# Joined sums of the block products written to PSUM; inverse sums, scaling and norm placed in an element's first step

## The chip, the cores and the metric

The kernel runs on one core of a Trainium2 chip. The metric is the device time of one execution in microseconds (us), the median of several runs; lower is better.

The names of the engines in the profile: PE is TensorE (matrix products; PEld its weight loads), DVE is VectorE, ACT is ScalarE, POOL is GpSimd, and SP is the engine that issues nearly all DMAs. Each takes its instructions in the order in which the program lists them, so an instruction that waits holds up all those behind it on its engine.

## The reference

Two transformer blocks, one after the other, on x of 16 batch elements × 256 tokens × 256 channels, with a context of 256 × 192 for each element and a conditioning vector of 256. Both have a self-attention, a cross-attention to the context and a feed-forward network, each behind a modulated layer norm. The change lies in the first block's self-attention:

```python
def _attn(xq, ctx, wq, wkv, wo, bo):          # layer 0: 16 heads of 64
    q = _heads(xq @ wq)
    k, v = jnp.split(ctx @ wkv, 2, axis=-1)
    k, v = _heads(k), _heads(v)
    q, k = _rope(q, sq, cq), _rope(k, sk, ck)
    sim = jnp.einsum('bhnd,bhmd->bhnm', q, k) * DH ** (-0.5)
    a = jax.nn.softmax(sim, axis=-1)
    o = jnp.einsum('bhnm,bhmd->bhnd', a, v)
    return o.transpose(0, 2, 1, 3).reshape(...) @ wo + bo
attn_in = _adaln(x, cond, ...)                 # layer norm, then scale and shift from cond
x = _attn(attn_in, attn_in, sa_wq, sa_wkv, sa_wo, sa_bo) + x
```

## The kernel before

All of x stays in SBUF. The program runs phase by phase (self-attention, cross-attention and feed-forward of layer 0, then of layer 1), in each phase element by element, and an attention element in two steps, `s = 0` and `s = 1` (here: the first and the second step). One step handles half of the heads: two groups of four heads, `u = 2s` and `2s + 1`. The order of the instructions on every engine is written out by hand in the main loop; a small framework adds the waits that the data and the reuse of buffers need. PSUM is one tile `banks` of eight banks of 128 × 512 floats, addressed by number.

At the end of each step `scores` (line 679 for the products, 694 for the exponentials on ACT) computes the transposed scores of the next step: group 0 in banks 0 to 3, group 1 in banks 4 to 7, and exponentials of two banks at a time. The sums of the softmax are not taken on PE: DVE adds the two key tiles (`stage_t`, `both`, line 703), transposes in blocks of 32 (`stage_turn`, `squares`, line 709) and reduces (`stage_reduce`, `rows`, line 716). The division comes one element later: `late` is the element before. `sum_up` (line 720 on) finishes its sums on PE with the matrix `fold`, inverts them on DVE (line 725), writes them to DRAM (`sums_seen`, line 728) and reads them back by four DMAs spread over 32 partitions each (`spread`, line 731); `scale` (line 740) multiplies the unscaled outputs by them on POOL, four instructions of 128 × 512. Then `fold_inner` (line 1031) prepares sums of blocks for the output projection, seven block products in place of eight, which `finish_folded` runs in the second step in banks 4 and 5, adding to x on DVE (lines 1045 to 1054).

The projections of queries and keys for the next step are also made as seven block products in place of eight (`seven`, from `by_seven` on: all elements but the first), over combinations of weights (`fold_projections`) and of token halves (`fold_tokens`, four POOL instructions, lines 593 to 596). Products 1 and 5 are started in banks 0 and 1 right behind the scores (`begin_seven`), ACT copies bank 0 into bank 2 (line 616), and further products are accumulated: banks 0, 1 and 2 are `first`, `fifth` and `chain`. Two states of `chain` are kept by ACT in SBUF (`keep_sum`, line 624, tile `kept`), and DVE later adds `fifth` to each (`add_fifth`, line 628). `rotate` applies the rotary embedding to one block (head half, token half): two DVE products with the cosines and sines (line 637, tiles `m0` and `m1`, two buffers each) and two POOL instructions that combine them into `qk` (line 643). A step has four rotations.

The layer norm of an element is split in time over three elements: `prepare_moments` (statistics on DVE; POOL's power, line 356), `prepare_norm` (two DVE scalings, line 364, two block transposes, line 374, four DMAs to DRAM, line 379, and two POOL additions of the bias to x, line 452) for the element `third`, `prepare_fetch` (four DMAs back, line 389) for `after`, and `prepare_input` (modulation by ACT, line 422, and POOL, line 426). `layer0_values` computes the values of the next element (`nxt`) in four banks, copied out by ACT (line 508).

Of the kernel before, what the change touches and what calls it, by code (L numbers as in the profile page):

```python
# [10 lines left out]
F32 = mybir.dt.float32  # L11
I32 = mybir.dt.int32
AF = mybir.ActivationFunctionType
ALU = mybir.AluOpType
AX = mybir.AxisListType

P = 128
N = 256
D = 256
# [4 lines left out]
NT = N // P  # L24
# [19 lines left out]
def fast(ctx: ExitStack, tc: tile.TileContext, a: dict, out: bass.AP, flag):  # L44
# [215 lines left out]
        return src.rearrange("(c p) m -> p c m", p=p)  # L260

    def broadcast_row(src, tag, name):
        t = wpool.tile([P, D], F32, tag=tag, name=name)
        nc.sync.dma_start(out=t, in_=src.partition_broadcast(P))
        return t

    def wtile(shape, tag, name, bufs=1):
        return wpool.tile(shape, F32, tag=tag, name=name, bufs=bufs)
# [219 lines left out]
    def layer0_values(job):  # L488

        w, key, kT = job["phase"]["w"], job["key"], job["kT"]  # L490
        job["v"] = work.tile([P, NT, H * 64], F32, tag="v", name=f"v_{key}")
        halves = [slice(half * 512, (half + 1) * 512) for half in range(2)]
        places = [[bank(6 - 2 * t + half, 512) for half in range(2)] for t in range(NT)]
        for t in range(NT):
            for pv, cut in zip(places[t], halves):
                for k in range(1 if job["cross"] else 2):
                    product(pv, kT[:, k, t * P : (t + 1) * P], w["wv"][:, k, cut], k == 0, k == 1)
        for t in range(NT if job["cross"] else 0):
            for g in range(2):
                for half, (pv, cut) in enumerate(zip(places[t], halves)):  # L500
                    r, m = slice(64 * half, 64 * half + 64), slice(64 * g, 64 * g + 64)
                    nc.tensor.matmul(  # L502
                        pv[m], kT[r, 1, t * P + 64 * g : t * P + 64 * g + 64], w["wv"][r, 1, cut],
                        start=False, stop=True,
                    )
        for t in range(NT):
            for pv, cut in zip(places[t], halves):
                nc.scalar.copy(job["v"][:, t, cut], pv)  # L508
# [78 lines left out]
    def fold_tokens(job, eng):  # L587

        b = [[job["hT"][:, k, t * P : (t + 1) * P] for t in range(NT)] for k in range(KC)]
        t1, t2, t3, t4 = (  # L590
            t for i in range(2) for t in wtile([P, 2, P], "bv", f"tokens{i}_{job['key']}", 2).rearrange("p i n -> i p n")
        )
        eng.tensor_tensor(t1, b[0][1], b[0][0], ALU.subtract)
        eng.tensor_tensor(t2, b[1][1], t1, ALU.subtract)
        eng.tensor_tensor(t3, b[1][1], b[0][1], ALU.subtract)
        eng.tensor_tensor(t4, b[1][0], t2, ALU.subtract)
        job["tokens"] = {1: b[0][0], 2: b[1][0], 3: b[1][1], 4: t4, 5: t1, 6: t2, 7: t3}
# [26 lines left out]
        nc.scalar.copy(kept, bank(2, 4, P))  # L624
        return kept

    def add_fifth(kept):
        nc.vector.tensor_tensor(kept, bank(1, 4, P), kept, ALU.add)  # L628

    def rotate(job, s, e, t, src):  # L630

# [572 lines left out]
    for i, (j, s) in enumerate(steps):  # L1204
# [123 lines left out]
        elif layer0:  # L1328
            then = attention(i + 1, 0)
            if leaving and s == 1 and nxt["kind"] == "ffn":  # L1330
                fold_input_weights(nxt["phase"], nc.gpsimd)
            if by_seven(then):
                ahead = then
                first, fifth, chain = (bank(n, 4, P) for n in range(3))
                for p in range(2):
                    stage_t(job, 2 * s, p)
                stage_turn(job, 2 * s)
                if late is not None and s == 1:
                    fold_inner(late, nc.gpsimd, 7, 6)
                if make_mod:  # L1340
                    make_mod["mod"] = make_mod["make_mod"](6)
                stage_t(job, 2 * s + 1, 0)
                layer0_sums(job, 2 * s, 4, (0,))
                seven(*ahead, 2, first)
                rotate(*ahead, 0, 0, first)
                seven(*ahead, 6, chain)
                two = keep_sum(*ahead, 0)
                if late is not None and s == 0:
                    sum_up(late, 6)
                stage_reduce(job, 2 * s)  # L1350
                layer0_sums(job, 2 * s, 4, (1,))
                stage_t(job, 2 * s + 1, 1)
                layer0_sums(job, 2 * s + 1, 5, (0,))
                seven(*ahead, 7, chain)
                three = keep_sum(*ahead, 1)
                layer0_sums(job, 2 * s + 1, 5, (1,))
                seven(*ahead, 4, chain)
                add_fifth(three)
                rotate(*ahead, 1, 1, three)
                seven(*ahead, 3, fifth)  # L1360
                add_fifth(two)
                rotate(*ahead, 0, 1, two)
                rotate(*ahead, 1, 0, chain)
                if leaving and s == 0:
                    load_phase(job["p"] + 1, "last")
                stage_turn(job, 2 * s + 1)
                if late is None or s == 0:
                    stage_reduce(job, 2 * s + 1)
            else:
                stage_t(job, 2 * s, 0)  # L1370
                stage_t(job, 2 * s, 1)
                stage_turn(job, 2 * s)
                rotary(then, 0, 0)
                stage_t(job, 2 * s + 1, 0)
                rotary(then, 0, 1)
                if late is not None and s == 1 and then:
                    fold_inner(late, nc.gpsimd, 7, 6)
                if late is not None and s == 0:
                    sum_up(late, 6)
                if make_mod:  # L1380
                    make_mod["mod"] = make_mod["make_mod"](6)
                stage_t(job, 2 * s + 1, 1)
                rotary(then, 1, 0)
                rotary(then, 1, 1)
                if leaving and s == 0:
                    load_phase(job["p"] + 1, "last")
                for e in range(2):
                    layer0_sums(job, 2 * s + e, 4 + e if then else e)
                stage_reduce(job, 2 * s)
                stage_turn(job, 2 * s + 1)  # L1390
                stage_reduce(job, 2 * s + 1)
            if late is not None and s == 1:
                if then:
                    finish_folded(late, (4, 5), (lambda: stage_reduce(job, 3)) if by_seven(then) else None)
                else:
                    finish(late, 7)
            if late is not None and s == 0:
                if job["p"] == 0 and not nxt["cross"]:
                    fold_tokens(nxt, nc.gpsimd)
                scale(late)  # L1400
                if nxt["kind"] == "attn":
                    fold_inner(late, nc.gpsimd, 5, 2, 1)
            if nxt["kind"] == "attn" and s == 0:
                layer0_values(nxt)
            if s == 0:
                prepare_moments(third)
                context_moments(third)
                prepare_fetch(after)
            else:
                if job["p"] == 0 and job["b"] == 0:  # L1410
                    fold_projections(job["phase"], 1, nc.vector)
                prepare_norm(third)
                prepare_context(third)
                prepare_input(after)
                if job["b"] == 0:
                    fold_weights(job["phase"])
        else:
            then = attention(i + 1, 1)
            at = 4 * s
            if s == 0:  # L1420
                prepare_fetch(after)
            if then:
                stage_a(then[0], then[1], at)
            if nxt["kind"] == "ffn" and s == 1:
                ffn_products(nxt, 0, at)
            for e in range(2):
                layer1_sums(job, s, e, at + 2 + e)
                if s == 1:
                    finish(prev, at + 1, (e,))
                elif nxt["kind"] == "attn":  # L1430
                    layer1_values(nxt, at + 1, e)
            if s == 0 and prev["kind"] == "attn":
                invert(prev)
                show_sums(prev)
                normalize(prev)
            if s == 0:
                prepare_moments(third)
            else:
                prepare_norm(third)
                prepare_input(after)  # L1440
                if job["cross"] and job["b"] == 5:
                    fold_input_weights(phases[job["p"] + 1], nc.gpsimd)
# [624 lines left out]
```

## Time and profile before

| | |
|---|---|
| median of 3 runs | 2209.86 us (2208.7 to 2212.47) |
| the profiled execution | 2207.08 us, span 2205.3 us |
| busy share of the span | PE 98%, PEld 67%, DVE 82%, POOL 60%, ACT 42% |
| granted TensorE clock | 0.999 |
| chain that ended last | PE 74%, DVE 15%, POOL 5%, issue 3% |
| self-attention of layer 0, elements 1 to 12 | second step 22.8 us, first step 20.3 us, from the starts of `begin_seven` |

Busy shares are means over the whole span. A group line names line, engine, operation, output and inputs, shape, count, then durations. A line of the timeline has start, length, engine, line, operation and count; the bracket gives the idle time of the engine just before and what ended it. A line of the chain of waits has start, length and the work that the end waited for at that time. The difference between the time of an execution and its span (1.8 us here) lies around the profiled instructions.

### The profile page before, as it was taken

What the parts mean: (1) busy time and instruction counts of PE and PEld (TensorE: products, weight loads), DVE (VectorE), ACT (ScalarE), POOL (GpSimd) and SP (SyncE); (2) the same over time, 40 slices, a digit from 0 to 9 for tenths busy, and PEclk for the clock granted to TensorE, in tenths of its full rate; (3) what the DMA queues carried; (4) which work ended last, traced back from release to release, by engine and by line L of the source; (5) the groups of instructions that cost most, each with busy time, mean ns of one, the idle gap of its engine ahead of it and who ended that gap; (6) DMA issues with size and microseconds to landing.
All of it is one profiled execution on the core that took longest, in us unless ns stands there. A gap on an engine that the chain in (4) does not pass through costs nothing.

```text
span 2205.3 us, 116296 instructions
## 1 busy us (share of the span) xinstructions
PE 2152.0 (98%) x52992; PEld 1471.8 (67%) x52992; DVE 1805.7 (82%) x3176; ACT 923.7 (42%) x1452; POOL 1332.6 (60%) x1362
## 2 busy tenths in 40 slices
PE   9899999999999999999999999999999999999999
PEld 5666677677676666665666666877665656666888
DVE  6998898898998999888888887775677777777875
ACT  3333433433343333323333333443566666665342
POOL 5867776776677776776767676673223223225763
PEclk9999999999999999999999999999999999999999
DMA  5111001101123221212121123221211232223221
GB/s 191 25 28 37 23 23 38 27 23 28 41 54 92 58 73 41 59 35 65 34 54 46 36 56 94 68 45 32 57 41 42 51 96 56 59 57 80 69 67 38
DMA packets 307054, 118.06 MB, mean 54 GB/s; under 512 B 243364, under 2 KB 289784, under 8 KB 306424
## 3 DMA queue, kind: packets, MB, share of 16 engines
q1 hardware_dynamic: 306008, 110.02, 20.2%
q8 instruction: 416, 6.82, 1.3%
q14 instruction: 86, 0.70, 0.1%
q10 hardware_dynamic: 544, 0.52, 0.1%
HBM read 77.14 MB, written 33.29 MB: 50 GB/s over the span
## 4 chain that ended last, share of the span: by engine, by line
PE 74%; DVE 15%; POOL 5%; issue 3%; DMA 1%; ACT 1%; SPq 0%; DVEq 0%; POOLq 0%; ACTq 0%
PE banks L82 47%; PE banks L679 13%; PE banks L751 7%; PE banks L770 5%; DVE m L637 5%; DVE both L703 3%; DVE squares L709 2%; PE banks L535 1%; PE banks L502 1%; POOL folded L956 1%; POOL folded L1031 1%; POOL raw L740 1%; DVE rows L716 1%; DVE kept L628 1%; ACT pr L694 1%
## 5 line engine op out<-in xcount | busy, mean ns | idle before, releaser
L694 ACT ACTIVATE pr<-banks 128x1024 f32<-128x1024 f32 x576 | 492.5, 936 | 487.7 <-PE banks L679 380.0
L703 DVE TENSOR_TENSOR both<-pr 128x512 f32<-128x512 f32 x256 | 267.2, 1061 | 55.8 <-ACT pr L694 52.4
L679 PE MATMUL banks<-qk 32*64 32x256 f32 x8192 | 255.1, 380 | 26.6 <-DVE x L1054 17.9
L643 POOL TENSOR_TENSOR qk<-m,m 128x256 f32<-128x256 f32 x240 | 194.7, 840 | 131.3 <-DVE m L637 126.4
L564 POOL TENSOR_TENSOR qk<-m,m 128x512 f32<-128x512 f32 x136 | 184.8, 1380 | 134.5 <-DVE m L556 115.4
L679 PEld LDWEIGHTS banks<-qk 32*64 32x64 f32 x8192 | 187.3, 132 | 98.5 <-DVE x L1054 25.6
L751 PE MATMUL banks<-pr,v 128*32 128x256 f32 x4096 | 244.6, 379 | 0.0
L556 DVE TENSOR_TENSOR m<-banks,rope 128x512 f32<-128x512 f32 x272 | 172.3, 679 | 48.8 <-POOL qk L564 45.8
L751 PEld LDWEIGHTS banks<-pr,v 128*32 128x32 f32 x4096 | 131.1, 110 | 72.4 <-ACT pr L694 0.7
L761 ACT COPY raw<-banks 128x512 f32<-128x512 f32 x128 | 75.1, 587 | 247.5 <-PE banks L751 241.4
L740 POOL TENSOR_TENSOR raw<-raw,spread 128x512 f32<-128x512 f32 x128 | 169.2, 1355 | 13.9 <-DMA spread<-sums_seen 12.4
L812 POOL TENSOR_TENSOR oT<-oT,spread 128x256 f32<-128x256 f32 x64 | 45.7, 736 | 206.1 <-DVE spread L811 206.1
L709 DVE STREAM_TRANSPOSE squares<-both 128x1024 f32<-128x1024 f32 x128 | 158.9, 1241 | 3.4
L716 DVE TENSOR_REDUCE rows<-squares 128x32 f32<-128x1024 f32 x128 | 154.5, 1207 | 1.7
L452 POOL TENSOR_TENSOR x<-x,bo_b 128x256 f32<-128x256 f32 x96 | 72.7, 778 | 120.2 <-DVE xh L364 120.2
L508 ACT COPY v<-banks 128x512 f32<-128x512 f32 x128 | 70.4, 593 | 170.4 <-PE banks L82 107.0
L1031 POOL TENSOR_TENSOR folded<-raw,raw 128x512 f32<-128x512 f32 x90 | 135.7, 1535 | 2.4
L770 PE MATMUL banks<-pr,wide_v 128*32 128x256 f32 x2048 | 134.3, 379 | 0.0
L82 PE MATMUL banks<-hT,wq_ca 128*32 128x256 f32 x2048 | 133.9, 379 | 0.0
L987 DVE TENSOR_TENSOR x<-banks,x 128x256 f32<-128x256 f32 (+2 forms) x150 | 79.7, 531 | 63.8 <-PE banks L82 57.7
L356 POOL TENSOR_TENSOR rstd<-ve,neg_half 128x2 f32<-128x2 f32 x95 | 68.6, 722 | 99.3 <-DVE ve L354 95.8
L679 PE MATMUL banks<-q,k 32*64 32x256 f32 x4096 | 127.7, 381 | 0.0
(266 smaller groups left out, 4569.6 us busy)
## 6 DMA issues: line engine op xcount, KB each, us to landing
turned<-blocks SPq DMA_DIRECT2D x380, 64.0 KB
fetched<-turned SPq DMA_DIRECT2D x380, 64.0 KB
spread<-sums_seen SPq DMA_DIRECT2D x128, 128.0 KB
x<-in_x SPq DMA_DIRECT2D x16, 256.0 KB
fetched_c<-turned_c SPq DMA_DIRECT2D x64, 64.0 KB
cT<-in_ctx_turned SPq DMA_DIRECT2D x16, 256.0 KB
out<-x SPq DMA_DIRECT2D x15, 256.0 KB
ctx<-in_ctx SPq DMA_DIRECT2D x16, 192.0 KB
```

The costliest lines, as they stand in the source:

```text
L82: nc.tensor.matmul(out[cut], lhsT[:, cut], rhs, start=start, stop=stop, **more)
L556: nc.vector.tensor_tensor(m, pq, rope[:, s : s + 1, :].to_broadcast([P, 2, N]), ALU.mult)
L564: nc.gpsimd.tensor_tensor(r, x, y, (ALU.subtract, ALU.add)[out])
L643: nc.gpsimd.tensor_tensor(r[:, :, t * P : (t + 1) * P], cos[:, i], sin[:, 1 - i], (ALU.subtract, ALU.add)[i])
L679: nc.tensor.matmul(banks[64 * g : 64 * g + 64, at + h, t * N : (t + 1) * N], lhs, rhs, start=(half == 0 and (t == 0 or job["layer"] == 1)) ...
L694: nc.scalar.activation(pr[:, one], sc[:, one], AF.Exp, scale=0.125 if job["layer"] == 0 else 0.25)
L703: nc.vector.tensor_tensor(job["both"][:, 2 * p : 2 * p + 2, :], pr[:, :, 0, :], pr[:, :, 1, :], ALU.add)
L709: nc.vector.transpose(job["squares"].rearrange("p b k -> p (b k)"), job.pop("both").rearrange("p h n -> p (h n)"))
L716: nc.vector.tensor_reduce(job["rows"][:, u, :], job.pop("squares"), AX.X, ALU.add)
L740: nc.gpsimd.tensor_tensor(part, part, spread[:, u : u + 1, :].to_broadcast([P, 2, N]), ALU.mult)
L751: nc.tensor.matmul(o[32 * h : 32 * h + 32, half, :], v[:, t, col : col + 32], prs[h // 2][:, h % 2, t, :], start=(t == 0), stop=(t == NT - 1),
L770: nc.tensor.matmul(o[32 * h : 32 * h + 32], v[:, t, 4 * c + h, 32 * e : 32 * e + 32], prs[h // 2][:, h % 2, t, :], start=(t == 0), stop=(t ...
```

## The change

- `add_fifth` writes its result to a PSUM bank (7 or 3) and `rotate` reads it there, no longer from `kept` in SBUF.
- In the steps with seven products, `sum_up` of the element before, `fold_tokens` of the next one and `scale` go from the end of the first step to its beginning: `sum_up` and `fold_tokens` ahead of `stage_turn`, `scale` behind the first rotation. `prepare_moments` goes to the same place, and `prepare_norm` from the second step to the end of the first.
- The reduction of the first group goes behind the rotations.
- `layer0_values` uses banks 4, 5, 6, 7 in this order, before 6, 7, 4, 5. The token sums have four buffers, before two.

```diff
 def broadcast_row(src, tag, name):
-        t = wpool.tile([P, D], F32, tag=tag, name=name)
+        t = wpool.tile([P, D], F32, tag=tag, name=name, bufs=4 if tag == "bv" else 2)
...
 def layer0_values(job):
-        places = [[bank(6 - 2 * t + half, 512) for half in range(2)] for t in range(NT)]
+        places = [[bank(4 + 2 * t + half, 512) for half in range(2)] for t in range(NT)]
...
 def fold_tokens(job, eng):
-            t for i in range(2) for t in wtile([P, 2, P], "bv", f"tokens{i}_{job['key']}", 2).rearrange("p i n -> i p n")
+            t for i in range(2) for t in wtile([P, 2, P], "bv", f"tokens{i}_{job['key']}", 4).rearrange("p i n -> i p n")
...
-    def add_fifth(kept):
-        nc.vector.tensor_tensor(kept, bank(1, 4, P), kept, ALU.add)
+    def add_fifth(kept, at):
+        out = bank(at, 4, P)
+        nc.vector.tensor_tensor(out, bank(1, 4, P), kept, ALU.add)
+        return out
...
             if by_seven(then):
                 for p in range(2):
                     stage_t(job, 2 * s, p)
+                if s == 0:
+                    if late is not None:
+                        sum_up(late, 6)
+                    if not nxt["cross"]:
+                        fold_tokens(nxt, nc.gpsimd)
                 stage_turn(job, 2 * s)
...
                 rotate(*ahead, 0, 0, first)
+                if s == 0:
+                    prepare_moments(third)
+                    if late is not None:
+                        scale(late)
                 seven(*ahead, 6, chain)
                 two = keep_sum(*ahead, 0)
-                if late is not None and s == 0:
-                    sum_up(late, 6)
-                stage_reduce(job, 2 * s)
                 layer0_sums(job, 2 * s, 4, (1,))
...
                 seven(*ahead, 4, chain)
-                add_fifth(three)
-                rotate(*ahead, 1, 1, three)
+                rotate(*ahead, 1, 1, add_fifth(three, 7))
                 seven(*ahead, 3, fifth)
-                add_fifth(two)
-                rotate(*ahead, 0, 1, two)
+                rotate(*ahead, 0, 1, add_fifth(two, 3))
                 rotate(*ahead, 1, 0, chain)
                 if leaving and s == 0:
                     load_phase(job["p"] + 1, "last")
+                stage_reduce(job, 2 * s)
                 stage_turn(job, 2 * s + 1)
...
             if late is not None and s == 0:
-                if job["p"] == 0 and not nxt["cross"]:
-                    fold_tokens(nxt, nc.gpsimd)
-                scale(late)
+                if not by_seven(then):
+                    scale(late)
                 if nxt["kind"] == "attn":
                     fold_inner(late, nc.gpsimd, 5, 2, 1)
             if nxt["kind"] == "attn" and s == 0:
                 layer0_values(nxt)
             if s == 0:
-                prepare_moments(third)
+                if by_seven(then):
+                    prepare_norm(third)
+                else:
+                    prepare_moments(third)
                 context_moments(third)
                 prepare_fetch(after)
             else:
...
-                prepare_norm(third)
+                if "moments" in third:
+                    prepare_norm(third)
```

## The prediction

> **What bounds the kernel now.** The page gives TensorE (PE) 98% of the span and the chain that ended last 74% PE, 15% VectorE (DVE). These are means over six phases; the change touches the layer-0 self-attention (about 50 to 690 us), so I read one element of it, from one start of `begin_seven` to the same start an element later: 351.28 to 394.44, the same to 0.05 us for ten elements running. Busy time by engine in its two steps, the second step (s=1) first:
>
> ```profile
> 351.28:374.12 22.84, 20.57 (x649) 16.99 (x641) 22.43 (x28) 7.50 (x11) 18.99 (x19) 1.00 0.02 4
> 374.12:394.44 20.32, 20.32 (x496) 13.00 (x489) 16.10 (x25) 8.82 (x13) 12.31 (x16) 1.00 0.23 56
> ```
>
> Columns: length, then PE, PEld, DVE, ACT, POOL busy, the granted clock (full), DMA. In the second step DVE is full (22.43 of 22.84). In the first PE is full (20.32 of 20.32), and DVE and POOL have 4 and 8 us spare. The chain of waits over the same stretch says where each rules:
>
> ```profile
> 361.43 2.11 DVE m L637 x2
> 363.54 0.61 DVE kept L628
> ...
> 364.25 3.47 DVE m L637 x4
> ...
> 371.73 0.43 DVE x L1054
> 372.16 0.04 issue
> 372.21 1.98 PE banks L679 x62
> ...
> 382.21 8.66 PE banks L82 x128
> 390.87 1.96 PE banks L679 x64
> ```
>
> Up to 372.2 the chain is DVE without a break, and the second half of the scores (L679) waits 1.67 us for the last addition to x (L1054). Then it is PE through the values to the next scores. So a DVE gain counts in the second step only, and any wait of PE in the first step counts in full. What rotation costs, by source line:
>
> ```profile
> L637 DVE TENSOR_TENSOR m<-banks,rope x120: 672/678/694, 53.6 to 690.5; 128x512 f32<-128x512 f32 x120
> L637 DVE TENSOR_TENSOR m<-kept,rope x116: 683/1131/1766, 58.4 to 668.6; 128x512 f32<-128x512 f32 x116
> ```
>
> Reading PSUM it is steady at 0.68; reading `kept` in SBUF it is 0.68 only while POOL is idle. And the timeline of the first step, for what is moved:
>
> ```profile
> 375.80 1.03 ACT L694 ACTIVATE pr<-banks 128x1024 f32<-128x1024 f32 x1
> 379.56 0.34 SPq L728 DMA_DIRECT2D sums_seen<-inv  x1
> 381.05 3.07 SPq L731 DMA_DIRECT2D spread<-sums_seen  x4
> 386.79 2.81 POOL L643 TENSOR_TENSOR qk<-m,m 128x256 f32<-128x256 f32 x4 [0.63 <-DVE m L637]
> 391.34 5.44 POOL L740 TENSOR_TENSOR raw<-raw,spread 128x512 f32<-128x512 f32 x4
> ```
>
> POOL scales (L740) after its last rotation; the spread sums had landed long before.
>
> **The change, part by part.** Differences are for one element.
>
> *Joined sums in PSUM.* `add_fifth` still reads a bank and `kept`, with 0.68 (L628). Its output in PSUM has no row on DVE; ACT's copies took 0.57 to PSUM (L616) and 0.59 to SBUF (L624), so I bound it at 0.6 to 0.8 and take 0.68. In the second step the two pairs of rotations that read `kept` now take 2.03 and 2.19 from start to start; the pair from a bank takes 1.20. Gain: 0.83 + 0.99 = 1.82 of DVE on the chain. In the first step it shortens work that nobody waits for.
>
> [...]
>
> *The first reduction behind the rotations.* In the second step PE waits 1.06 for `add_fifth` (361.38, releaser L628). A reduction of 1.13 ahead of it is moved back, so that wait goes. But the chain at 372.2 is the sum of DVE's work, which the move leaves as it is: worth nothing beside the 1.82.
>
> *`sum_up` at the head of the first step.* Its product goes to bank 6, which the last exponential reads until 376.83 (row above). PE is through with `begin_seven` at 375.78 and now meets this product first: it waits 1.05 + 0.05. All PE work of the step lies behind it: +1.1. (The product's own 0.14 only moves.) DVE's reciprocal stands before the transpose and waits as well, to about 377.4; DVE's spare time covers that, since `rotate(0,0)` ends at 380.7 instead of 379.3 and the next PE wait on DVE (`add_fifth` before product 3) is met with 0.1 to spare.
>
> *`scale` between the rotations.* The reciprocal ends at about 377.75. From the issue of the sums' write to the end of the last spread issue the rows of twelve elements have 3.2 to 5.1, mean 4.1. When that lands is not seen in this phase, since POOL comes later; in the cross-attention POOL waited for it, until 2.7 to 3.6 after the last issue. Bounds 5.9 to 8.7; I take 4.1 + 2.9 = 7.0, because the queue ahead of it is now empty but the path is the same. Landing at 384.8. POOL then scales for 4 × 1.24 = 4.96, to 389.75, and only then does three rotations of 1.39 each: 391.1, 392.5, 393.9. The first half of the scores needs the second of these: 392.5. PE is ready at 390.8 + 1.1 = 391.9. So the first step grows by 1.1 + 0.6 = 1.7.
>
> [...]
>
> *The buffers of `m`.* `m` has two buffers per tag, so the fourth rotation on DVE waits until POOL is through with the second. That was at 386.2, in time; now it is 391.1. DVE stands still for some 4 us, rotates until 392.4, and then has reduction, transpose, reduction and the moved norm: 1.13 + 1.2 + 1.13 + 0.65 + 0.75 = 4.9, to 397.3. The next step begins at 392.5 + 3.64 = 396.15 and its first `both` stood 0.53 before that, at 395.6: DVE enters its full step 1.65 late. By then POOL has come further, so the `both` additions, 1.55 to 1.8 each beside POOL, meet it less; between nothing and 1.6 comes back, I take 0.8.
>
> *The rest.* `prepare_norm` (1.5 us on DVE, two POOL additions of 0.74, four writes on SP) leaves the end of the second step, where DVE afterwards had 0.68 to wait for PE anyway: no gain. On SP the four fetches stand behind those writes now; the fetched tile is wanted some 8 us later. `prepare_moments` (1.2) and `fold_tokens` (4 × 0.45) fall into spare time of DVE and POOL; the extra token buffers make that legal. `layer0_values` takes banks 4 and 5 first: in self-attention the copy out of bank 5 ended 0.85 before the values; in cross-attention it ends 0.84 after their start, when PE reaches bank 5 at 0.86: some 0.05 for each of 15.
>
> Sum for one element: first step +1.7, second −1.82 + 1.65 − 0.8 = −1.0, together +0.7; for 13 elements +9. The ends: the very first step gains 1.8; element 14's SP queue lands at 8.4 (+1.4); in element 15 the write lands behind 1 MB of weights (5.3 instead of 1.5, 10.2 in all, +7 for its scores), of which the next step, where DVE stood 3.74 waiting for POOL, gives back about half: together +3. In all +12 on the profiled execution's 2207.1 (span 2205.3 and 1.8 around it), which is 2.8 under the median: 2209.9 + 12 = 2222.
>
> **The rivals.**
> *Faster.* The spread lands at the short end (5.9) and all of the 1.6 comes back: first step +1.1, DVE enters 1.2 late, second step −1.82 + 1.2 − 1.2 = −1.8, so −0.7 each, −9 and nothing at the ends: 2200. For it: DVE fills the second step, and the gain of 1.82 is the best measured number here. Against: 8 of the 16 scalings in the cross-attention began only as the spread landed, 7.0 to 8.2 after the write. Should DVE also get back to PE's own limit (22.84 − 1.06 − 1.67 = 20.1), it would be −1.6 each: 2189.
> *No change.* The same two terms cancel at a landing of 6.3 or so: 2210.
> *Much slower.* One mechanism, POOL's queue behind the DMA: from 6.4 upward every further us of landing is a us of the first step. At 8.4, which element 14 has, the first step costs +3.1 and with nothing of the late DVE given back the second −0.2: +2.9, and 13 × 2.9 = 38: 2248. At 7.6 it is 2238.
> *It does not do what it says*: if the rotations from the added banks still took 1.0 rather than 0.68, the 1.82 would be 0.5, 17 more: inside that range.
>
> **How the numbers follow.** About 0.2% (4.4 us) can be told from no change. Forecast, POOL's and DVE's late work ahead of the DVE gain: 0.46, 2222. Much slower 0.14, together 0.60 slower. Faster 0.24, no change 0.16. The range takes the landing from 5.9 to 7.6: 2200 to 2239. The likeliest case alone lies at 2215 to 2232.
>
> **What would show it.** Right: L637 steady at 0.68 in all forms; PE waiting about 1.1 on ACT's exponential before the product with `fold`; POOL L740 idle on the spread DMA in most elements; DVE L637 waiting some 4 us on POOL L643 once per element; first steps near 22.0, second near 21.9. Wrong: first steps of 21.4 (landing early), or second steps under 21 (DVE no longer late).

## The result and the profile after

The changed kernel takes 2235.49 us (median of 4 runs, 2233.42 to 2240.81) against 2210.97 for the kernel before on the same chip (4 runs, 2208.70 to 2212.47): 1.0116 times as long, 95% interval 1.0094 to 1.0137. It is 24.5 us slower. The forecast was 2222, slower by 12, range 2200 to 2239: the direction and the chain of causes came out, the size is half of what was measured. The profiled execution of the changed kernel is the slowest of its four (2240.81, span 2239.0), that of before is 3.9 under its median, so the two profiles lie 33.7 apart, not 24.5. The sums below keep to that.

All lines of the changed part have numbers higher by 2 now (L637 is L639, L679 is L681, L740 is L742). From here on a step is counted from ACT's copy of bank 0 into bank 2 (L616), which starts 1.2 us behind the start of `begin_seven`. In elements 3 to 13 of this kernel the lengths from either mark agree within 0.02. The two steps of one element, second step first, columns as before:

```profile
409.55:431.52 21.97, 20.41 (x648) 17.17 (x644) 19.74 (x28) 7.43 (x11) 13.39 (x18) 1.00 0.13 28
431.52:453.37 21.85, 21.04 (x496) 13.26 (x492) 15.54 (x24) 9.02 (x14) 15.09 (x16) 1.00 0.10 27
```

DVE is no longer full in the second step (19.74 of 21.97; before, counted from the same copy, 22.39 of 22.84), and that step became 0.86 us shorter. PE is no longer full in the first step (21.04 of 21.85, before 20.33 of 20.33), and that step became 1.5 us longer here, 2.0 in the mean over elements 3 to 13. The rotations by source line, now all from PSUM:

```profile
L639 DVE TENSOR_TENSOR m<-banks,rope x240: 675/682/696, 54.6 to 718.5; 128x512 f32<-128x512 f32 x120
```

The 1131 ns median of the form that read `kept` is gone. The chain of waits over the same element (start, length, work) still goes through DVE in the second step and through PE in the first:

```profile
415.58 1.28 DVE m L639 x2
416.87 0.60 DVE both L705
417.47 0.62 DVE banks L629
...
420.18 2.48 DVE m L639 x4
...
428.41 2.02 PE banks L681 x62
...
433.09 0.27 PE banks L82 x8
...
439.43 8.66 PE banks L82 x128
448.10 4.14 PE banks L681 x128
```

DVE had less to do in the second step and yet rules it, because it enters late. Why is in the timeline of the first step and in the waits between 90 and 635 us (total us, times, longest):

```profile
433.09 0.27 PE L82 MATMUL banks<-fold,rows 128*32 128x32 f32 x8 [0.81 <-ACT pr L696]
433.87 0.34 SPq L730 DMA_DIRECT2D sums_seen<-inv  x1
435.38 2.66 SPq L733 DMA_DIRECT2D spread<-sums_seen  x4
437.01 1.43 POOL L645 TENSOR_TENSOR qk<-m,m 128x256 f32<-128x256 f32 x2 [10.32 <-DVE m L639]
440.76 5.02 POOL L742 TENSOR_TENSOR raw<-raw,spread 128x512 f32<-128x512 f32 x4 [1.14 <-DMA spread<-sums_seen]
445.73 4.25 POOL L645 TENSOR_TENSOR qk<-m,m 128x256 f32<-128x256 f32 x6
447.19 1.29 DVE L639 TENSOR_TENSOR m<-banks,rope 128x512 f32<-128x512 f32 x2 [3.80 <-POOL qk L645]
```

```profile
DVE m L639 <- POOL qk L645: 58.5, 13, 5.8
DVE inv L727 <- PE banks L82: 41.2, 12, 3.5
PEld banks L681 <- POOL qk L645: 22.2, 13, 5.5
POOL raw L742 <- DMA spread<-sums_seen: 21.1, 12, 3.1
```

PE waits for ACT before the product with `fold`; SP writes the sums and reads them back; POOL stands before the scaling until the spread lands; the last rotations on POOL stand behind 5 us of scaling; PE waits for them before the scores, and DVE for the buffer of `m`. The signs that the prediction named as right are there, with PE's wait at 0.81 rather than 1.1.

With L for the time from the issue of the sums' write to POOL's first scaling, the first step measures L + 14.94, within 0.02, for each of the elements 2 to 13: 2.34 from its start to the write, L, 5.0 of scaling, 2.8 of two rotations, and 4.8 to the next start. The prediction's own steps make L + 15.02. L is 6.61 to 8.31 in elements 3 to 13, mean 7.38.

### The profile page after: what moved, and what is told of

It is laid out like the page before. It is cut to its first block, busy times and chain, and to the rows that moved or that the text cites. A ratio compares the mean times of both kernels' runs of the same rounds, so it can differ in the third digit from the quotient of the medians.

```text
span 2239.0 us, 116245 instructions
## 1 busy us (share of the span) xinstructions
PE 2162.0 (97%) x52992; PEld 1475.0 (66%) x52992; DVE 1754.6 (78%) x3176; ACT 926.8 (41%) x1452; POOL 1290.7 (58%) x1362
## 4 chain that ended last, share of the span: by engine, by line
PE 74%; DVE 11%; POOL 6%; DMA 3%; issue 3%; ACT 2%; SPq 1%; DVEq 0%; POOLq 0%; ACTq 0%
PE banks L82 44%; PE banks L681 15%; PE banks L753 7%; PE banks L772 5%; DVE m L639 3%; POOL raw L742 2%; PE banks L535 1%; DMA spread<-sums_seen 1%; PE banks L502 1%; DVE squares L711 1%; POOL folded L958 1%; DVE rows L718 1%; ACT pr L696 1%; DMA sums_seen<-inv 1%; POOL qk L645 1%
## 5 line engine op out<-in xcount | busy, mean ns | idle before, releaser
L645 POOL TENSOR_TENSOR qk<-m,m 128x256 f32<-128x256 f32 x240 | 173.4, 749 | 209.3 <-DVE m L639 208.8
L681 PE MATMUL banks<-qk 32*64 32x256 f32 x8192 | 260.6, 383 | 30.5 <-POOL qk L645 18.8
L681 PEld LDWEIGHTS banks<-qk 32*64 32x64 f32 x8192 | 193.5, 133 | 102.3 <-POOL qk L645 32.4
L705 DVE TENSOR_TENSOR both<-pr 128x512 f32<-128x512 f32 x256 | 224.7, 890 | 33.0 <-ACT pr L696 30.3
L639 DVE TENSOR_TENSOR m<-banks,rope 128x512 f32<-128x512 f32 x240 | 153.1, 685 | 79.5 <-POOL qk L645 72.8
L556 DVE TENSOR_TENSOR m<-banks,rope 128x512 f32<-128x512 f32 x272 | 172.4, 680 | 44.9 <-POOL qk L564 41.7
L742 POOL TENSOR_TENSOR raw<-raw,spread 128x512 f32<-128x512 f32 x128 | 161.2, 1295 | 38.2 <-DMA spread<-sums_seen 34.5
L681 PE MATMUL banks<-q,k 32*64 32x256 f32 x4096 | 127.7, 381 | 0.0
```

Of the source, the lines that this page charges most:

```text
L639: nc.vector.tensor_tensor(m, src, rope[:, i : i + 1, t * P : (t + 1) * P].to_broadcast([P, 4, P]), ALU.mult)
L645: nc.gpsimd.tensor_tensor(r[:, :, t * P : (t + 1) * P], cos[:, i], sin[:, 1 - i], (ALU.subtract, ALU.add)[i])
L681: nc.tensor.matmul(banks[64 * g : 64 * g + 64, at + h, t * N : (t + 1) * N], lhs, rhs, start=(half == 0 and (t == 0 or job["layer"] == 1)) ...
L705: nc.vector.tensor_tensor(job["both"][:, 2 * p : 2 * p + 2, :], pr[:, :, 0, :], pr[:, :, 1, :], ALU.add)
L742: nc.gpsimd.tensor_tensor(part, part, spread[:, u : u + 1, :].to_broadcast([P, 2, N]), ALU.mult)
```

## The experiments

Theory: the PSUM write is a gain of some 2 us per element, and moving `sum_up` and `scale` ahead costs more than that, through POOL's queue behind the spread DMA and through DVE's late entry into the second step. Rivals: the cost lies in PE's wait for ACT's exponential; in the other moved pieces (moments, norm, token sums, first reduction); or the PSUM write itself gains nothing. The steps are those of elements 3 to 13, mean or steady value, in the profiled execution; before has 20.32 and 22.84, the changed kernel 22.32 (mean) and 21.98. For e4 the second number is the steady one; the mean is 24.03.

| kernel | us, median (range) | ratio to before, 95% | first / second step |
|---|---|---|---|
| e1_scale_last | 2198.56 (2195.76 to 2200.67) | 0.9948 (0.9933 to 0.9962) | 21.34 / 20.83 |
| e2_sums_scale_back | 2184.49 (2181.99 to 2188.02) | 0.9887 (0.9869 to 0.9905) | 20.32 / 20.83 |
| e3_psum_only | 2175.25 (2174.20 to 2175.91) | 0.9842 (0.9829 to 0.9856) | 20.32 / 20.53 |
| e5_own_buffer | 2215.93 (2213.29 to 2217.91) | 1.0029 (1.0019 to 1.0040) | 21.83 / 20.83 |
| e11_reduce_back | 2173.43 (2170.95 to 2174.91) | 0.9835 (0.9822 to 0.9848) | 20.85 / 19.66 |
| e14_norm_second | 2171.79 (2168.49 to 2173.12) | 0.9826 (0.9812 to 0.9839) | 20.85 / 19.58 |
| e4_sums_in_sbuf | 2278.37 (2269.30 to 2282.78) | 1.0300 (1.0279 to 1.0321) | 23.68 / 24.62 |
| e7_sum_behind | 2234.98 (2233.55 to 2236.35) | 1.0117 (1.0101 to 1.0132) | 22.24 / 21.97 |
| e12_weights_later | 2236.07 (2232.80 to 2239.82) | 1.0105 (1.0090 to 1.0121) | 22.23 / 21.98 |
| e15_moments_last | 2166.77 (2163.98 to 2169.25) | 0.9796 (0.9783 to 0.9809) | 20.35 / 20.00 |
| e16_weights_later | 2172.55 (2168.46 to 2173.49) | 0.9819 (0.9806 to 0.9833) | 20.33 / 20.00 |

**Scaling back at the end.**

```diff
                 rotate(*ahead, 0, 0, first)
                 if s == 0:
                     prepare_moments(third)
-                    if late is not None:
-                        scale(late)
...
             if late is not None and s == 0:
-                if not by_seven(then):
-                    scale(late)
+                scale(late)
```

> The changed kernel with scale back at the end of the first step; sum_up stays at its head. Theory P (POOL's queue): the scaling ahead of three rotations makes the first step as long as the landing of the spread sums plus 14.9 us, and makes DVE enter the second step late. Then the first step here is 21.4 in every element (20.3 + 1.1 for PE's wait before the product with fold), the second 20.4 to 21.1, elements 1 and 15 lose their extra 5 and 7: about 2198 (2192 to 2204). Rival Q (PE's wait): the product at the head of the step is the cost; then the first step stays near 22 and the time near 2230.

Measured 2198.56, 37 us under the changed kernel and under before too. The place of the scaling alone decides the sign. The second step is 20.83 in place of 21.98, since DVE enters it in time; the first is 21.34, which is 20.32 + 1.02: with POOL's wait gone, PE's wait for the exponential is what remains, as the theory priced it (1.1). In e1's timeline POOL now scales last, without a wait, and PE's wait is there as in the changed kernel:

```profile
414.60 0.27 PE L82 MATMUL banks<-fold,rows 128*32 128x32 f32 x8 [0.81 <-ACT pr L696]
427.75 5.09 POOL L742 TENSOR_TENSOR raw<-raw,spread 128x512 f32<-128x512 f32 x4
```

**Sums back as well, and only the PSUM write left.** The next takes e1 and puts `sum_up` back behind `keep_sum`:

```diff
                 if s == 0:
-                    if late is not None:
-                        sum_up(late, 6)
...
                 two = keep_sum(*ahead, 0)
+                if late is not None and s == 0:
+                    sum_up(late, 6)
```

> The changed kernel with scale and sum_up both back at their old places; sums in PSUM, norm, moments, token sums and the first reduction stay as changed. Theory P with the PE wait of 1.1 as a second term: first step 20.3, second 20.4 to 21.1, about 2185 (2176 to 2192), so 13 to 16 below the kernel with scale alone put back. If the wait at the head is hidden: no difference to that kernel. Rival R (the sums in PSUM bring nothing): 2200 to 2210.

The third also puts token sums (with two buffers), moments, norm and first reduction back: what is left of the change is `add_fifth` into a bank and the banks' order in `layer0_values`.

> The kernel before with only the joined sums in PSUM and the order of the banks for the values. From the prediction's 1.82 us of DVE in the second step: second step 21.0, first 20.3, 2184 (2180 to 2192). Rival R (a DVE result in PSUM costs more, or DVE is not what ends the second step): 2205 to 2215.

e2: 2184.49, 14 less, and the first step is 20.32 again. e3: 2175.25, 9 less than e2 and 9 less than expected. So the other moved pieces cost time in sum, and the PSUM write is worth more than the prediction gave it: 22.84 − 20.53 = 2.31 per second step, not 1.82. The banks' order, which e3 keeps too, was not taken alone. What PE waits for in e3's second step is only this:

```profile
427.93 1.08 PE L82 MATMUL banks<-hT,sums_of_weights 128*32 128x128 f32 x32 [0.51 <-DVE banks L629]
```

**Buffers for the last rotation.** The changed kernel, with the fourth rotation's `m` in a buffer of another tag, so that DVE does not have to wait for POOL:

```diff
-            m = work.tile([P, 4, P], F32, tag=f"m{i}", name=f"m{i}_{key}_{u}_{t}")
+            last = e == 1 and t == 0 and (job["b"] < NB - 1 or s == 0)
+            m = work.tile([P, 4, P], F32, tag="cT" if last else f"m{i}", name=f"m{i}_{key}_{u}_{t}")
```

> The changed kernel, but the fourth rotation's two products have buffers of their own (the idle pair of the kept states), so that DVE does not wait until POOL has done the second rotation. Theory P says two separate costs: the first step stays at landing + 14.9 (22.3 in the mean), since PE waits for POOL's third rotation; DVE no longer enters the second step late: 20.4 to 21.1 instead of 21.9. So 2222 (2216 to 2228). If DVE's lateness costs nothing: 2235.

Measured 2215.93, 19.6 under the changed kernel: more than expected. The second step is 20.83, the same as in e1, so DVE's lateness costs 1.15 us of it. The first step also falls, to the greater of 21.34 and about L + 14.6 (14.58 to 14.67 where L decides). Why it falls by these 0.35 was not followed up. DVE's wait is the one cost of the three (PE's wait, POOL's queue, DVE's buffers) that goes without moving anything.

**Sums left in SBUF.** The changed kernel without the PSUM write:

```diff
     def add_fifth(kept, at):
-        out = bank(at, 4, P)
-        nc.vector.tensor_tensor(out, bank(1, 4, P), kept, ALU.add)
-        return out
+        nc.vector.tensor_tensor(kept, bank(1, 4, P), kept, ALU.add)
+        return kept
```

> The changed kernel with the joined sums in SBUF again, all else as changed. By the run with the sums in PSUM alone (2.3 us off each second step): first step still landing + 14.9 (22.3 in the mean), second step about 24 instead of 21.98: 2262 (2252 to 2270). If the sums in PSUM only help while POOL is late, as in the kernel before: 2235 to 2245.

Measured 2278.37, 16 above what was expected: 43 us is what the PSUM write saves in the new order, so it cannot be the cause of the loss. What was missed lies in the first step, where the rotations from `kept` now run beside the scaling:

```profile
466.09 2.38 DVE L638 TENSOR_TENSOR m<-kept,rope 128x512 f32<-128x512 f32 x2
466.36 6.62 POOL L741 TENSOR_TENSOR raw<-raw,spread 128x512 f32<-128x512 f32 x4 [0.70 <-DMA spread<-sums_seen]
```

The scaling takes 6.6 in place of 5.0, the first step is L + 15.8 to L + 16.7 in nine of elements 3 to 13 in place of L + 14.9, and its mean of 23.68 against the 22.3 expected makes 15 us over the eleven. The second step came out near the 24 expected (mean 24.03), but not for the reason given: behind PE's waits for x the granted clock falls in it (0.62 in the window below). Here are the timeline, and the window of this kernel from that product on (length, PE, PEld, DVE, ACT, POOL, clock, DMA):

```profile
452.82 2.90 PE L680 MATMUL banks<-qk 32*64 32x256 f32 x62 [1.21 <-DVE x L1055]
452.82:456.50 3.68, 3.68 (x78) 2.53 (x82) 1.14 (x2) 0.77 (x1) 0.00 (x0) 0.62 0.02 4
```

The same 62 products took 1.98 before at full clock. With the first two projection groups behind them (1.08 and 0.93, in place of 0.65 and 0.62) that is 1.7 us beyond the waits themselves. The lower clock is there in nine of the eleven second steps, which take 24.5 to 24.6; the other two take 21.4 and 21.5.

**Sums one product later.** The changed kernel with `sum_up` behind the first half of the values of group 0, so that PE works while the exponential ends:

```diff
                 if s == 0:
-                    if late is not None:
-                        sum_up(late, 6)
...
                 layer0_sums(job, 2 * s, 4, (0,))
+                if late is not None and s == 0:
+                    sum_up(late, 6)
                 seven(*ahead, 2, first)
```

> The changed kernel with sum_up one product group later on PE (behind the first half of the first group's sums), so that PE has work while the last exponential runs; the product with fold still starts as that exponential ends. If PE's wait of 1.1 and POOL's wait for the landing lie side by side (theory: the first step is the longer of 20.3 + what PE waits and landing + 14.9): no change, 2235 (2230 to 2239). If they add, as the prediction's sum 1.1 + 0.6 reads: 0.8 us less per first step, 2224.

Measured 2234.98: nothing. The first step is L + 14.93 in most elements, as before the edit, because the write leaves at the same moment (2.34 after the start of the step). (Elements 3 and 14 take 25.3 and 25.1: PE's waits of 2.40 and 2.26 there are followed by a granted clock of 0.74 and 0.66.) PE no longer waits for the exponential; it waits for POOL before the scores instead:

```profile
431.28 0.27 PE L82 MATMUL banks<-fold,rows 128*32 128x32 f32 x8
446.37 4.34 PE L681 MATMUL banks<-qk 32*64 32x256 f32 x128 [0.95 <-POOL qk L645]
```

So PE's wait lies beside the way of the sums, not ahead of it. Only the longer of the two counts.

**The first reduction.** e2 with the first group's `stage_reduce` in its old place:

```diff
                 if late is not None and s == 0:
                     sum_up(late, 6)
+                stage_reduce(job, 2 * s)
...
                     load_phase(job["p"] + 1, "last")
-                stage_reduce(job, 2 * s)
```

> As the kernel with sums and scale both back, and the first reduction back ahead of the second group's addition. In that kernel DVE stands 1.17 us before add_fifth waiting for ACT's kept state, a hole into which the reduction of 1.13 fits. If the move of the reduction opened the hole (theory): x is done 1.1 earlier, PE alone ends the second step, 19.6 to 19.8 instead of 20.83, first step 20.32: 2171 (2166 to 2176). If the reduction is worth nothing, as the prediction had it: 2184.

Measured 2173.43, 11.1 under e2. The second step goes from 20.83 to 19.66. What the reduction had filled in its old place is seen in e2's timeline, where DVE stands idle before `add_fifth`:

```profile
431.57 0.70 DVE L629 TENSOR_TENSOR banks<-banks,kept 128x512 f32<-128x512 f32 x1 [1.17 <-ACT kept L624]
442.64 1.98 PE L681 MATMUL banks<-qk 32*64 32x256 f32 x62 [0.69 <-DVE x L1056]
```

DVE waits there for ACT's copy, then does the 1.2 us of reduction later, on the chain, and PE waits for the addition to x. The first step, however, grew by 0.53: the moments (1.2) and the reduction together now delay `add_fifth`.

**The norm and the moments.** The next leaves the norm in the second step, as before; the one after it puts `prepare_moments` back to the end of the first step too.

```diff
             if s == 0:
-                if by_seven(then):
-                    prepare_norm(third)
-                else:
+                if not by_seven(then):
                     prepare_moments(third)
```

> As the kernel before this one in the list (sums, scale and reduction back), and the norm back at the end of the second step too. The prediction: the norm's place is worth nothing, since DVE waits for PE behind it in either place: the same time within 3 us. If the norm's move to the first step is a part of the gain: 1.5 us per second step, some 20 us more.

```diff
-                if s == 0:
-                    prepare_moments(third)
...
             if s == 0:
-                if not by_seven(then):
-                    prepare_moments(third)
+                prepare_moments(third)
```

> e14_norm_second with prepare_moments moved to the end of the first step; against the kernel before this leaves only the sums in PSUM, the banks' order and the token sums ahead with four buffers. Theory: the moments (1.2 us on DVE) and the first reduction delay add_fifth by 0.5 us in the steps of e11 and e14; without them the first step is again 20.3 us, the second 19.6 to 20.0, and the time about 2164 us (2160 to 2169). Rival: the place of the moments is worth nothing, and the time stays at 2172.

With the scaling back, the norm's place is worth nothing that can be told (2171.79 against 2173.43); no run moved the norm alone in the changed kernel, where DVE is late. The moments' place is worth about 5: 2166.77, first step 20.32 again, at the price of 0.4 in the second. This is the fastest kernel of the study, 0.9796 of before. Beside the PSUM write and the banks' order it keeps one moved piece, the token sums ahead with four buffers. That piece separates it from e3: ratio 0.9796 against 0.9842, with intervals apart. The prediction had it fall into spare time; the second step is 20.00 with it and 20.53 without, and element 1's first step 22.07 against 24.94. In the windows of the fastest kernel, counted as above, PE is full again or nearly so:

```profile
415.04:435.05 20.01, 19.88 (x648) 16.99 (x644) 19.56 (x29) 7.26 (x11) 15.51 (x17) 1.00 0.04 7
435.05:455.38 20.33, 20.33 (x496) 13.01 (x492) 16.54 (x24) 8.99 (x14) 14.61 (x18) 1.00 0.22 53
```

**Element 1.** Its first step took 30.64, before 22.03 (the 20.3 of the table ahead holds from element 2 on). In the changed kernel's timeline the five products that fold the phase's weights stand on POOL ahead of everything:

```profile
74.44 7.20 POOL L1024 TENSOR_TENSOR folded_w<-wo_sa 128x512 f32<-128x512 f32 x5
83.39 1.42 POOL L645 TENSOR_TENSOR qk<-m,m 128x256 f32<-128x256 f32 x2
92.51 5.85 PE L681 MATMUL banks<-qk 32*64 32x256 f32 x128 [4.63 <-POOL qk L645]
```

The first edit moves them to the end of that step; the second does the same in the fastest kernel.

```diff
             if s == 0:
...
                 prepare_fetch(after)
+                if job["b"] == 1 and job["p"] == 0:
+                    fold_weights(job["phase"])
             else:
...
-                if job["b"] == 0:
+                if job["b"] == 0 and job["p"] > 0:
                     fold_weights(job["phase"])
```

> The changed kernel, with phase 0's folding of weights on POOL (five products, 7.2 us) moved from the end of element 0 to the end of element 1's first step. Theory: element 1's first step is 30.6 us long, 8 more than the others, because these products stand on POOL ahead of its first rotation; then the step becomes 23 to 25 us, the second step of element 1 about 2 longer (23), and the kernel takes about 2230 us (2226 to 2233). Rival: the queues and weight loads of the kernel's start make the step long; then it stays at about 30 and the time at 2235.

> e15_moments_last with phase 0's folding of weights moved as in e12_weights_later. Theory: element 1's first step, some 25 us in e2 and e3, falls to between 20.5 and 22, and the time is about 2161 us (2157 to 2166). Rival: POOL's lateness there is hidden behind other waits once the sums are in PSUM, and the time stays at e15's.

The cause was right and the cure was not. Element 1's first step falls from 30.64 to 24.67, where the theory had 23 to 25, but its second grows from 20.83 to 25.18, element 0's second from 16.87 to 19.70 and element 2's first from 23.80 to 25.35: 92.1 in all before the edit, 94.9 behind it, and the time stays (2236.07). In e12 PE waits in the second step now, for a DVE addition:

```profile
106.51 1.54 PE L82 MATMUL banks<-hT,sums_of_weights 128*32 128x128 f32 x32 [2.80 <-DVE banks L629]
```

In e16 element 1's first step hardly changes (22.07 in e15, 21.71 here: the 25 that the expectation started from belong to e2 and e3), its second goes from 20.45 to 26.64, and the kernel is 5.8 slower than e15: both accounts of the time were wrong there. In neither of the two places tried did POOL have 7 us free in the first two elements.

## Why the prediction was right or wrong

**Right.** The landing behind the earlier `scale`, POOL's scaling ahead of the last rotations, DVE's stall on the buffers, DVE's late entry and the gain of the PSUM write all appear in the profile, and e1, e5 and e4 take three of them away one by one. The length of the first step as a function of the landing was off by 0.08. That the norm's move brings no gain was right (e14), but in the changed kernel it lies on DVE's late path (below). `add_fifth` into a bank took 0.70 in the median (L629), where 0.68 had been taken. The rotations from a bank took 682 ns in the median (L639), where 683 was the least from `kept` before, and e3 gains 2.31 per element, more than the 1.82.

**Where the sum failed: the sizes.** The mechanism held; the terms that failed are four, each taken up below: the landing of 7.0, element 1 costed like any other, element 15's loss of 7 of which the next step "gives back about half", and PE's clock behind long waits (0.55 and 0.50, below), for which the sum has no term and gives no reason. A fifth, DVE's lateness of 1.65, was too small as well and was hidden by luck. By the two profiled executions 33.7 stand against 12:

| | forecast | measured |
|---|---|---|
| elements 3 to 13, first step | +18.7 | +22.0 |
| elements 3 to 13, second step | −11 | −9.8 |
| elements 0, 1, 2, 14 | +1.0 | +6.3 |
| element 15 and all after it | +3.5 | +14.2 |
| start, up to the first step | 0 | +1.0 |

*The landing*, 7.0 in the prediction, measured 7.38 in the mean, 6.61 at the least. Four rows of elements 3 to 13 are above 8.0, and they make the mean: the other seven have 6.95. The prediction put the long landings only into elements 14 and 15; element 14, given 8.4, had 6.61.

*Element 1*: forecast like any other, measured +8.6 and −3.5 in its two steps. The prediction costed the moved DVE and POOL work, but did not look at what stood in POOL's queue ahead of it in the one element where the queue is full: 7.2 us of weights and 1.8 of token sums. And behind PE's wait of 4.63 the granted clock was 0.55 (below), and the scores took 2.1 longer. Element 2 had L = 8.86, +2.6 in all.

*Element 15*: the write and spread took 10.78, as forecast (10.2). PE waited 5.25 for them, and then the scores themselves took longer (timeline, then the window, columns as above):

```profile
718.55 6.84 PE L681 MATMUL banks<-qk 32*64 32x256 f32 x128 [5.25 <-POOL qk L645]
718.50:725.30 6.80, 6.75 (x128) 5.98 (x128) 6.73 (x10) 1.94 (x2) 6.77 (x8) 0.57 0.01 2
```

Before, these 128 products took 3.71 at full clock. From the start of `begin_seven` to the end of these scores the step lost 9.6, not 7: 6.5 up to their start, near the forecast, and 3.1 in the scores themselves, for which the sum has no term. "Gives back about half" failed too: the next step gave back 1.2, not 3.5. DVE's 3.74 there had stood beside PE's own work. PE's waits of that step (0.54, 0.16, 0.98 and 0.31 before) went, but a stall of 1.59 that the profile calls issue came. The distance of the two kernels at the first product behind that step's scores (718.98 before, 746.98 after) was 28.0. The remaining 5.7 of 33.7 arise in phases where the code differs by nothing that matters. They stay unexplained; 9 of the 33.7 are the places of the two profiled executions among their runs.

*DVE's lateness.* DVE's first `both` of the second step stood 0.53 ahead of `begin_seven` before, and stands 2.33 behind it now (454.49 against 452.16, the same in elements 3 to 12): 2.86 late, not 1.65. The moved norm's two scalings, taken at 0.65, need 1.83 there:

```profile
452.06 1.83 DVE L364 TENSOR_SCALAR xh<-x,mv,rstd 128x256 f32<-128x256 f32 x2
454.49 2.92 DVE L705 TENSOR_TENSOR both<-pr 128x512 f32<-128x512 f32 x2
```

In e5 and e1 the first `both` is at −0.53 again, and the second step 1.15 shorter; so of 2.86 some 1.7 came back, not 0.8. That the second step as a whole came out near the forecast (−0.86 against −1.0) is luck in part. In time and with the reduction in its old place it takes 19.66 (e11), 3.18 under before, where the sum had 1.82; the reduction's move takes back 1.17 (e2: 20.83), where the sum had nothing, and the lateness 1.15, where it had 0.85. PE's own limit of 20.1 for that step was too high as well; e14 has 19.58.

*The form of the sum.* PE's wait (1.1) and POOL's lateness (0.6) were added; e7 shows that they lie side by side. The prediction reached the right 1.7 at its L because it had the write leave after the wait in any case, so this cost the number nothing, but the reading "1.1 of it is PE's" was wrong.

*Two terms set to nothing.* "Worth nothing" for the reduction behind the rotations fails once the sums are in PSUM: e11 gives 11 us back. Nor did the wait that it was to remove go; in the changed kernel it is 0.84, before 1.06:

```profile
418.13 1.08 PE L82 MATMUL banks<-hT,sums_of_weights 128*32 128x128 f32 x32 [0.84 <-DVE banks L629]
```

Token sums in spare time: worth some 8 us, as a gain. What these two are worth in the changed kernel as it stands, where DVE is late for a greater reason, no run shows.

The rival "much slower" had the mechanism right as well, by the same formula: it gave 2238 at a landing of 7.6. The measured kernel lies between it and the forecast.

## What to carry to other kernels

When an engine that still has spare time is given an earlier wait on a DMA, cost what stands behind that wait in its queue, and the buffers that the work behind it holds: here 5 us of scaling moved in front of three rotations cost 37 us, and one more pair of buffers gave 20 of them back. Split a change into its pieces before judging it: inside a change that loses 1.2%, three of the pieces (PSUM write, banks' order, token sums) gain 2.0%. A mean landing time is not enough for a term that repeats; take its spread, and look at the first and the last pass of the loop on their own.

## What the runs showed of the hardware

Some waits of PE cost more than their length here. In the changed kernel the granted clock over the 3.5 us behind PE's waits of 4.63 and 5.25 us was 0.55 and 0.50, and the scores behind them took 5.85 and 6.84, where 3.71 was the rule before at full clock. Shorter waits went either way: one of 3.02 at 63 us left the clock at 1.00 in the changed kernel, and behind that of 3.0 at the same place in e1 (62.66) it was 0.50; behind waits of 0.37 and 1.21, 1.8 us apart, it was between 0.54 and 0.66 in e4, while a pair of 0.64 and 1.21 left it at 1.00 in the kernel before (629.92 and 631.74); single waits of 1.75 and less left it at 1.00 in the changed kernel, and behind one of 1.62 it was 0.75 in e12 (139.33). What decides between these cases was not shown: all this was read from the traces, and no run varied it alone.

The sums' write of 16 KB was followed by its first spread issue 1.47 us later in most elements, but 2.5 to 3.7 later in four of elements 3 to 13 (7, 8, 12 and 13), those with L above 8. In each of them a fetch of instructions (16 KB, a queue of its own) falls into the transfer, and in none of the other seven; in the window of element 8's write, 388 to 394 us, the queues show it:

```profile
q1 hardware_dynamic: 252, 0.12, 7.6%
q8 instruction: 1, 0.02, 1.5%
```

That the fetch is the cause is argued from its place in time, and no run removed it.
